# Second pass of layer one in pairs of blocks: 29 products on streamed weight sums in place of 2 × 15 on resident ones

## The chip, the cores and the metric

The kernel runs on one core of one Trainium2 chip. The core has five engines that run their own instruction streams: TensorE (PE in the profile, its weight loads PEld), VectorE (DVE), ScalarE (ACT), GpSimd (POOL) and SyncE (SP), which here issues the DMAs. Measured is the device time of one execution, in microseconds (us). The kernel before takes 2706.76 us, the median of three runs (2703.83, 2707.84, 2706.76).

## The reference

The input x has 128 batch entries of 64 tokens with 768 channels. It is normalised per token and cut at zero; two graph layers follow, and x is added at the end. All of it is fp32. One layer, with h the tokens and weights W_left, W_right, W_lin (768 × 768):

```python
m_left = h @ W_left.T;  m_right = h @ W_right.T          # per token
u_left = h @ m_left.T / sqrt(768); u_right = h @ m_right.T / sqrt(768)   # 64 x 64 per batch entry
u = u_left * adj_tri + u_left * diag_mask + u_right * adj_tri.T
e = exp(u) * adj;  attention = e / (sum(e, axis=2) + 1e-10)
h_lin = h @ W_lin.T + b_lin
ctx = attention @ h_lin
h = relu(layer_norm(ctx, ln_a, ln_b))       # (z - mean) / (std + 1e-3) * a + b
```

## The kernel before

The tokens are worked on in 16 blocks of 512 (8 batch entries), or 8 pairs of blocks. A block is held transposed, channels on partitions. The 768 channels are three thirds of 256, each of two halves of 128 partitions. Both dense multiplications are done by a scheme that trades products for sums: a block's 512 tokens are two groups of 256, the channels three thirds in and three out, and in place of all the small products the kernel multiplies sums of weight slices by sums of token groups. A product is one weight sum (256 × 256) times one token sum (256 tokens), which is several matmuls into a PSUM bank, and the bank is added to or subtracted from several outputs.

Each layer has two passes.

*Pass one* (`pass_one`, L436) makes `m_left` and `m_right`, the scores and the attention. It works in pairs of blocks: 29 products (`PRODUCTS`, L116) of each kind, left and right (`project`, L520; its matmuls are L535). The weight sums were made once (`W_OPS`, 23 sums beyond the nine raw slices) and stand in DRAM, from where SP streams them into a ring of eight tiles (`stream`, L198). Token sums (`X_OPS`, 30 per pair) are made by POOL (`token_op`, L277) four products ahead. VectorE and ScalarE read the banks (`read`, L295; the sums L222 and L223).

*Pass two* (`pass_two`, L847) makes `h_lin`, the context and the normalisation. It works in single blocks: 15 products each (`ORDER`, L97; `linear`, L1055, matmuls L1069), with weight sums of W_lin that stay in SBUF in the tile ROOM all through the pass (15 slots), and 11 token sums a block on POOL (`T_SUMS`, L92). The bias is copied into each block's first banks by ScalarE ahead of the products (`fresh`, L838). In layer one (l = 0 in the code) the context of blocks 0 to 12 is made by `context_block` (L881, 16 matmuls, L900, in one place, after the next block's product 12) and normalised by `finish_block` (L964); those of blocks 13 to 15, and all of layer two, are made in two halves in two places (`context`, L867, matmuls L877; `finish`, L1011). Since the mean is taken out of W_lin, b_lin and with it of ctx beforehand (`centre`, L201), the normalisation needs only the sum of squares (ScalarE), its root, and an inverse (VectorE). The rows z are stored to DRAM for the next pass.

*What sets the order.* The program is written out in the order of its loops, and each engine runs its instructions in that order. Work that is not TensorE's is put between products in two ways: `put` gives a function a slot (pass one has four slots per pair of left and right product, 116 for a pair of blocks; a block of pass two has 30), and `idle` is a queue from which `run` (L75) takes one function at each slot where the plan has none. A function of the queue may be `None`, for a pause. The last pair of pass one, U = 7 of 0 to 7, has the queue of `one_aside` (L1143): eight pauses, then nine loads of slices of W_lin by SP (`load_n`, L152 to L154, into ROOM), `centre` (nine reductions L216, means, nine subtractions L219, all on VectorE), and the 17 sums `W_SUMS` on POOL that turn nine slices into the 15 of `ORDER`. The last two softmax chains, of blocks 14 and 15, follow the end of the pair. Pass two of layer one has the queue of `two_aside` (L1151): the raw loads of W_left and W_right of layer two, their sums on POOL, and stores of them to DRAM (L196).

SP's queue holds in order: the streams of pass one, the loads of tokens (1.5 MB a block), attention (128 KB), stores of rows (192 KB each) and weight sums (256 KB each). A copy on ScalarE (L565) holds SP back in U = 7 until 795 us.

## Time and profile before

| what | value |
|---|---|
| median of the three runs | 2706.76 us |
| the profiled execution, device time | 2705.84 us |
| its span | 2704.1 us |
| its mean granted TensorE clock | 0.998 |
| pass one, layer one | 0 to 891.5 us, TensorE busy 879.38 |
| pass two, layer one | 891.5 to 1357.3 us, TensorE busy 464.69 of 465.80 |
| pass one, layer two | 1357.3 to 2222 us, TensorE busy 863.52 |
| pass two, layer two | 2222 to 2704.1 us, TensorE busy 470.10 |

In the lines of the profile each entry names the line of the code, the engine, the operation, and the tiles: `X<-room,ts` is a write to PSUM bank X from the weight tile room and a token sum. A duration in microseconds follows, or in groups the number of instructions (x...), the busy time and the mean duration in ns. The windows show, for a stretch, the busy time of each engine with its number of instructions, then the granted clock, the share of the DMA engines that was busy, and GB/s. The stages end at the first product of the next one.

### The profile page before, as it was taken

The page shows a single profiled execution, that of the slowest core. Times are in us where ns is not written, and L with a number is a line of the kernel's source. Part 1 is how long each engine was busy: PE and PEld are TensorE (multiplying, and loading weights), DVE is VectorE, ACT ScalarE, POOL GpSimd, SP SyncE. Part 2 cuts the span into 40 slices and gives each one's busy share as a digit, 9 for nine tenths or more (in the row PEclk, how much of TensorE's full clock was granted, in tenths as well). Part 3 has the DMA queues.
Part 4 walks back from the last instruction along what each step waited for, and adds up shares of the span by engine and source line. Part 5 has one row for each costly group of instructions (what it writes and reads, how often), then busy time and mean ns, then how long its engine had stood idle before and what let it go on. Part 6 is the DMA issues. An engine that isn't in the chain of part 4 may idle for free.

```text
span 2704.1 us, 47306 instructions
## 1 busy us (share of the span) xinstructions
PE 2677.7 (99%) x18514; PEld 2301.3 (85%) x18514; DVE 1499.1 (55%) x2456; ACT 832.4 (31%) x1617; POOL 1381.4 (51%) x1071
## 2 busy tenths in 40 slices
PE   9999999999999999999999999999999999999998
PEld 8788888888888888888788888888888888888886
DVE  7664755756647433334344545546446475666667
ACT  4032131221310254454631221221212304445443
POOL 6633244333336765566433325335244286887886
PEclk9999999999999999999999999999999999999999
DMA  8886956858765345558594956968759524655655
GB/s 272 268 309 212 289 197 208 279 202 265 244 207 181 102 143 184 166 167 255 184 284 174 317 187 212 286 191 279 229 193 301 211 79 135 182 160 159 186 154 148
DMA packets 310222, 567.81 MB, mean 210 GB/s; under 512 B 62832, under 2 KB 190064, under 8 KB 301808
## 3 DMA queue, kind: packets, MB, share of 16 engines
q1 hardware_dynamic: 309840, 564.39, 64.9%
q8 instruction: 148, 2.42, 0.4%
q14 instruction: 74, 0.61, 0.1%
q10 hardware_dynamic: 160, 0.39, 0.0%
HBM read 429.40 MB, written 135.27 MB: 209 GB/s over the span
## 4 chain that ended last, share of the span: by engine, by line
PE 96%; DVE 1%; SPq 0%; issue 0%; DMA 0%; ACT 0%; DVEq 0%; ACTq 0%
PE right L535 17%; PE X L1069 12%; PE X L535 11%; PE V L535 11%; PE Z L535 9%; PE Y L535 9%; PE V L1069 8%; PE Y L1069 6%; PE both L474 5%; PE Z L1069 4%; PE aux L877 2%; PE aux L900 1%; PE Y L900 0%; PE Z L474 0%; DVE wp L223 0%
## 5 line engine op out<-in xcount | busy, mean ns | idle before, releaser
L223 POOL TENSOR_TENSOR ts<-ht 128x512 f32<-128x512 f32 x352 | 481.6, 1374 | 172.6 <-PE X L1069 69.6
L223 POOL TENSOR_TENSOR ts<-ht,ts 128x512 f32<-128x512 f32 x192 | 252.9, 1324 | 345.7 <-PE V L535 202.1
L535 PE MATMUL right<-ts,wp 128*128 128x252 f32 (+1 forms) x1632 | 380.9, 376 | 0.6 <-DVE wp L223 0.6
L535 PEld LDWEIGHTS right<-ts,wp 128*128 128x128 f32 x1632 | 310.0, 190 | 39.5 <-DVE wp L223 1.0
L483 POOL TENSOR_TENSOR wm<-adj,tri 128x256 f32<-128x256 f32 x60 | 42.3, 728 | 490.7 <-DMA wp<-ws 274.5
L223 DVE TENSOR_TENSOR m<-m,X 128x512 f32<-128x512 f32 x160 | 105.5, 684 | 257.9 <-ACT m L305 180.2
L223 DVE TENSOR_TENSOR m<-m,right 128x504 f32<-128x504 f32 (+1 forms) x304 | 199.5, 674 | 87.8 <-PE right L535 74.1
L1069 PE MATMUL X<-room,ts 128*128 128x256 f32 x1024 | 244.0, 380 | 0.2
L535 PE MATMUL Z<-ts,wp 128*128 128x256 f32 x992 | 234.3, 379 | 0.0
L223 POOL TENSOR_TENSOR ts<-ht,ht 128x512 f32<-128x512 f32 x128 | 163.2, 1285 | 137.8 <-PE right L535 92.8
L1069 PEld LDWEIGHTS X<-room,ts 128*128 128x128 f32 x1024 | 191.7, 190 | 31.7 <-issue 1.8
L535 PEld LDWEIGHTS Z<-ts,wp 128*128 128x128 f32 x992 | 188.4, 190 | 24.9
L535 PE MATMUL X<-ts,wp 128*128 128x256 f32 x872 | 207.5, 381 | 1.9 <-DVE wp L223 1.9
L535 PE MATMUL V<-ts,wp 128*128 128x252 f32 (+1 forms) x864 | 201.6, 376 | 0.0
L305 ACT ACTIVATE m<-right 128x504 f32<-128x504 f32 (+1 forms) x64 | 36.2, 592 | 506.8 <-PE both L474 486.8
L535 PEld LDWEIGHTS X<-ts,wp 128*128 128x128 f32 x872 | 164.4, 190 | 25.5 <-POOL ts L223 2.3
L382 ACT ACTIVATE ht<-ht,b_col,a_col 128x512 f32<-128x512 f32 x192 | 141.3, 806 | 140.9 <-DMA ht<-h 140.9
L1069 PE MATMUL Y<-room,ts 128*128 128x256 f32 x768 | 182.5, 379 | 0.0
L535 PEld LDWEIGHTS V<-ts,wp 128*128 128x128 f32 x864 | 164.2, 190 | 20.4
L1069 PEld LDWEIGHTS Y<-room,ts 128*128 128x128 f32 x768 | 145.8, 190 | 20.4 <-issue 0.6
L223 DVE TENSOR_TENSOR hl<-hl,V 128x512 f32<-128x512 f32 (+1 forms) x136 | 89.2, 656 | 128.9 <-PE V L1069 118.7
L223 DVE TENSOR_TENSOR m<-m,Y 128x512 f32<-128x512 f32 x144 | 95.8, 684 | 116.0 <-PE Y L535 105.2
(225 smaller groups left out, 4866.3 us busy)
## 6 DMA issues: line engine op xcount, KB each, us to landing
wp<-ws SPq DMA_DIRECT2D x435, 512.0 KB, 6.3
ht<-h SPq DMA_DIRECT2D x62, 1536.0 KB, 8.3
h<-room SPq DMA_DIRECT2D x112, 384.0 KB, 7.1
z<-z SPq DMA_DIRECT2D x128, 192.0 KB, 3.1
ws<-wp SPq DMA_DIRECT2D x93, 256.0 KB, 4.2
xr<-in_x_dram SPq DMA_DIRECT2D x120, 192.0 KB, 3.6
out_dram<-xr SPq DMA_DIRECT2D x120, 192.0 KB, 2.6
room<-z SPq DMA_DIRECT2D x112, 192.0 KB, 5.1
```

The source lines that it names most:

```text
L223: (eng.tensor_add if sign == "+" else eng.tensor_sub)(o, a, b)
L305: nc.scalar.activation(to(o), p, AF.Copy, scale=1.0 if sign == "+" else -1.0)
L382: nc.scalar.activation(ht, ht, AF.Relu, bias=cols[1][:, c:c + 1], scale=cols[0][:, c:c + 1])
L474: nc.tensor.matmul(p[h * S + e:h * S + e + 32, q, e:e + 95], ht[:, c, b * S + e:b * S + e + 32], mb[:, e:e + 95], start=(c == 0), stop=(c ...
L483: nc.gpsimd.tensor_tensor(wm[:, :, k], adj[:, :, 1 - k], tri[:, k].unsqueeze(1).to_broadcast([P, Q, S]), op=ALU.mult)
L535: nc.tensor.matmul(p[:, g], wk[:, c, g * P:(g + 1) * P], tk[:, c, :].rearrange("p (b s) -> p b s", s=S)[:, :, :ns], start=(new and g == c ...
L877: nc.tensor.matmul(cx[k][i, m, :HH], at[j, q, :], hl[j, q, m * HH:(m + 1) * HH], start=True, stop=True)
L900: nc.tensor.matmul(parts[r, k][n][i], at[j, q, :], hl[j, q, cut], start=True, stop=True)
L1069: nc.tensor.matmul(p[:, n], b[t][:, c, r * P:(r + 1) * P], w[s][:, c, :], start=(i in FIRST and i not in PRELOAD and n == c == 0), stop=(c ...
```

## The change

In pass two of layer one, blocks 0 to 13 are worked on as seven pairs with 29 products each (`PAIRS`), the same scheme as in pass one but with its own order and signs; blocks 14 and 15 keep `linear` with the 15 old sums.

- *Weights.* The 29 weight sums are made in the last pair of pass one: `pair_weights` replaces `sums_n` in the queue. Its functions are, in order: nine stores of raw (centred) slices, 23 sums alternately on POOL and VectorE, each with a store to DRAM where `PAIRS` uses it (`WN`, 29 tiles of 256 KB), then the 17 old sums on POOL with a pause after each and stores of the 15 results (`WO`), then the first nine streams. The pauses ahead of the loads are ten rather than eight. With `both`, `run` takes from the queue at every slot of this pair, also where the plan has something; in the pairs it does so at every second product.
- *Streams.* ROOM becomes a ring of nine slots of 256 KB (`NR`); after product n SP issues the load for product n + 9. The last nine of these, and `first_weights` in the last pair, bring the old sums back for blocks 14 and 15.
- *Token sums.* 30 per pair on POOL (`PAIR_OPS`), eight products ahead, in place of 2 × 11.
- *First reads and bias.* VectorE does all reads of the pairs' banks; the first read of an output adds or subtracts the bias (`read_biased`), in place of ScalarE's copy ahead and its first reads.
- *Context.* `context_block` and `finish_block` are gone. Each pair makes the four halves of the two blocks before it after its products 0, 4, 9 and 14, with `context` and `finish`.
- *Places.* The loads of tokens, attention and rows, and the transposes for layer two, are put at other slots; `h_lin` has a third buffer in ROOM.

The diff, cut to its core:

```diff
-    def run(slot):
-        if slot in plan:
-            for f in plan.pop(slot):
-                f()
-        elif idle:
+    def run(slot, both=False):
+        given = plan.pop(slot, ())
+        for f in given:
+            f()
+        if idle and (both or not given):
             f = idle.popleft()
...
+    PAIR_OPS = ((2, 12, "-", 3, 11), (2, 13, "-", 12, 1), (4, 14, "-", 5, 4), (4, 15, "-", 1, 14),
...
+    PAIRS = ((9, 9, "X", True, "+1+5"), (11, 4, "Y", True, "-8"), (3, 13, "V", True, "-5"),
...
+    WN = {w: dram.tile([P, K2, D], F32, name=f"wn{w}") for w in sorted({p[0] for p in PAIRS})}
+    WO = [dram.tile([P, K2, D], F32, name=f"wo{s}") for s in range(len(ORDER))]
...
+    NR = 9
+
+    def stream_n(n):
+        nc.sync.dma_start(single(n % NR), WN[PAIRS[n % len(PAIRS)][0]])
+
+    def pair_weights(own):
...
+        def keep(w):
+            if w in WN:
+                nc.sync.dma_start(WN[w], where[w])
+
+        def sums(n, eng):
+            _, o, sign, a, b = W_OPS[n]
+            t = where[o] = spare.popleft()
+            if sign == "neg":
+                eng.tensor_scalar_mul(t, where[a], -1.0)
+            else:
+                added(eng, t, sign, where[a], where[b])
+            keep(o)
...
+        for w in range(9):
+            idle.append(lambda w=w: keep(w))
+        for n in range(len(W_OPS)):
+            idle.append(lambda n=n: sums(n, (nc.gpsimd, nc.vector)[n % 2]))
...
+        def old(n):
+            o, s, a, b = W_SUMS[n]
+            added(nc.gpsimd, single(o), s, single(a), single(b))
+            keep_old(n)
...
+        idle.append(lambda: keep_old(-1))
+        for n in range(len(W_SUMS)):
+            idle.extend([lambda n=n: old(n), None])
+        idle.append(None)
+        for n in range(NR):
+            idle.append(lambda n=n: stream_n(n))
...
-                            run(2 * n)
+                            run(2 * n, l == 0 and U == NU - 1)
...
+            def read_biased(p, to, sign, j):
+                b = rows["bias", l][:, (4, 2, 0)[j]].unsqueeze(1).to_broadcast([P, 2, D])
+                if j == 0:
+                    (nc.vector.tensor_add(to, p, b) if sign == "+" else nc.vector.tensor_sub(to, b, p))
...
+            def pair(s, ends):
+
+                late, seen, bank = [], set(), {}
...
+                for i, (w, t, at, new, what) in enumerate(PAIRS):
+                    if new:
+                        bank[at] = ps_st.tile([P, 2 * TH], F32, name=at)
+                    p = bank[at].rearrange("p (r d) -> p r d", r=2)
+                    x, wt = tokens(l, s, t, 2), single((s * len(PAIRS) + i) % NR)
+                    for r in range(2):
+                        for c in range(K2):
+                            nc.tensor.matmul(p[:, r], x[:, c, r * P:(r + 1) * P], wt[:, c, :],
+                                             start=(new and r == c == 0), stop=(c == K2 - 1), skip_group_check=True)
+                        if r == 0:
+                            run(2 * i, i % 2)
...
+                        if o in seen:
+                            added(nc.vector, to, sign, to, pp)
+                        else:
+                            read_biased(pp, to, sign, j)
...
+                    n = s * len(PAIRS) + i + NR
+                    if n < (NU - 1) * len(PAIRS):
+                        stream_n(n)
...
+            def first_weights():
+                t = sp.tile([P, H // 32, Q, 32], F32, name="xb", bufs=1).rearrange("p b q j -> p (b q j)")
+                W[l, "n"] = {}
+                for n in range(6):
...
+            def pairs():
+                for s in range(NU - 1):
+                    for n in range(2):
+                        put(4 + 10 * n, lambda n=n: load_h(2, l, 2 * s + 2 + n))
+                        put(40 + 3 * n, lambda n=n: load_at(2 * s + n))
+                    put_pair_ops(s, "after", PAIR_SLOTS)
...
+                    if s == NU - 2:
+                        put(30, first_weights)
+                    if s in aside:
+                        aside[s]()
+                    ends = {}
+                    if s:
+                        ends = {e: ((2 * s - 2 + n // 2, n % 2), (2 * e + 6, 2 * e + 7, 2 * e + 8))
+                                for n, e in enumerate((0, 4, 9, 14))}
+                    pair(s, ends)
...
-            idle.extend(none * 8)
+            idle.extend(none * (8 if l else 10))
             later(load_n(l), 0)
             centre(l)
-            later(sums_n(l), 0)
+            if l:
+                later(sums_n(l), 0)
+            else:
+                own = sp.tile([P, 2 * H], F32, name="own", bufs=1)
+                pair_weights([own[:, n * K2 * D:(n + 1) * K2 * D].rearrange("p (c d) -> p c d", c=K2) for n in range(3)])
```

## The prediction

> **What bounds the kernel now.** I read the page first, then the chain that ended last, then the stage in question by time windows.
>
> ```profile
> span 2704.1 us, 47306 instructions
> PE 2677.7 (99%) x18514; PEld 2301.3 (85%) x18514; DVE 1499.1 (55%) x2456; ACT 832.4 (31%) x1617; POOL 1381.4 (51%) x1071
> PE 96%; DVE 1%; SPq 0%; issue 0%; DMA 0%; ACT 0%; DVEq 0%; ACTq 0%
> ```
>
> TensorE works 99% of the span and carries 96% of the chain: a matmul saved is time saved, if everything that feeds it stays ahead. Second pass, layer one (L0 in the code), runs from 891.5 to 1357.3 us. Windows (columns: length, then PE, PEld, DVE, ACT, POOL busy, clock, DMA share, GB/s):
>
> ```profile
> 840.00:850.00 10.00, 10.00 (x48) 8.80 (x47) 10.00 (x14) 0.00 (x0) 8.24 (x7) 1.00 0.59 202
> 891.50:1357.30 465.80, 464.69 (x2435) 379.55 (x2432) 176.53 (x323) 220.74 (x543) 284.13 (x226) 1.00 0.56 177
> 1130.00:1140.00 10.00, 10.00 (x48) 8.74 (x47) 3.19 (x5) 1.69 (x3) 3.09 (x3) 1.00 0.97 316
> 1280.00:1290.00 10.00, 10.00 (x66) 7.18 (x65) 5.93 (x9) 3.01 (x5) 3.82 (x3) 1.00 0.99 341
> ```
>
> The stage has room on DVE, ACT and POOL on average, and 177 GB/s of DMA on average; but there are stretches of 10 us where the DMA engines are full, at 316 to 341 GB/s. The first line lies before the stage, at the end of pass one: VectorE is full there already. The timeline of TensorE gives the prices of a product and of a context:
>
> ```profile
> 1023.85 1.89 PE L1069 MATMUL Y<-room,ts 128*128 128x256 f32 x8
> 1025.58 1.89 PE L1069 MATMUL V<-room,ts 128*128 128x256 f32 x8
> 1027.40 0.65 PE L900 MATMUL Y<-hl,at 64*64 64x512 f32 x2
> 1028.31 1.90 PE L900 MATMUL aux<-hl,at 64*64 64x256 f32 x24
> 1030.14 1.99 PE L1069 MATMUL Z<-room,ts 128*128 128x256 f32 x8
> ...
> 2308.96 1.89 PE L1069 MATMUL X<-room,ts 128*128 128x256 f32 x8
> 2310.78 1.52 PE L877 MATMUL aux<-hl,at 64*64 64x384 f32 x16
> 2312.23 1.99 PE L1069 MATMUL Z<-room,ts 128*128 128x256 f32 x8
> ```
>
> A product (8 records of 4 fp32 matmuls) starts every 1025.58 − 1023.85 = 1.73 us. A whole-block context takes 1030.14 − 1025.58 = 4.56; with the product after it (1.83 to the next), less two products (3.45), it costs 2.94 per block. The two-place form, which layer two has at 2308.96: 3.27 + 1.83 − 3.45 = 1.65 a place, 3.30 per block.
>
> **The change part by part.**
>
> *Products.* Seven pairs take 29 products in place of 30: −7 × 1.73 = −12.1 us. All of it lies on the path.
>
> *Context.* Blocks 0 to 12 leave the block form for two places: 13 × (3.30 − 2.94) = +4.7. Blocks 13 to 15 had two places already.
>
> *End of pass one, the part that decides.* In the last pair's run (U=7, starting about 784; a step, one kind of one product, is 1.73 us, 58 steps) the old kernel loads nine slices of W_lin, centres them and makes 17 sums on POOL. The new one makes 23 further weight sums, alternately on POOL and VectorE, each stored by SP, then the 17 old ones, each of the 15 survivors stored, then nine streams. It takes work from the idle queue at every slot, so the centring is pulled forward: to steps 12 to 21 from 823–862 us. The relevant rows:
>
> ```profile
> L154 SPq DMA_DIRECT2D room<-in_w_lin_dram x9: 367/384/537, 775.6 to 818.4; - x9
> DMA to landing us min/median/max: 2.7/8.3/10.7
> L219 DVE TENSOR_TENSOR room<-room,wmm x9: 679/850/1780, 838.7 to 861.2; 128x512 f32<-128x512 f32 x9
> PE Z L1069 <- DVE wp L490: 1.1, 2, 0.6
> ```
>
> VectorE between steps 12 and 38 (26 × 1.73 = 45 us): reads of PSUM 26 × 0.62 (the spacing of its reads) = 16; two blocks' softmax pieces 6.5; centring nine reduces at 0.68, nine subtractions (9.4 together in this trace, 0.68 to 1.78 each), three means, 18 with their gaps; 11 weight sums at 1.05 (the nine subtractions' mean, as they too run beside POOL) 11.5. Sum 52. Waits in order: the first reduces stand at step 12, about 804, while SP, held by a copy until 795, issues its slices at about 1 us each until 803.5, and they land 8.3 later: about 4 lost. The alternating sums make DVE wait for POOL and back: some 3. So 58 against 45, 13 behind. Reads of PSUM queue behind this on VectorE, and TensorE waits for the banks that they free: the banks let it run 2 or 3 steps (3 to 5 us) ahead, so it is about 9 late. Lower bound 0 (subtractions at 0.68, slices landing in 2.7: demand 45); upper 13.
>
> That lateness moves POOL too. From the end of the VectorE jam (about 862) POOL still owes the 17 old sums, the last 8 or so token sums of U=7, seven of the first pair and two blocks' masks: 33 × 1.23 (spacing of its sums in the row of 17) = 40 less what overlaps: the last old sum ends about 898. In the kernel before it ended at 893.8 and TensorE began pass two at 891.5, waiting only 0.6 for Z. Now the first streamed weight stands on SP behind the store of that last sum, and lands 4 later (a 256 KB store's 4.2, below): product 0 at about 902 against 891.5 = +10.5, less the small gap at 894 that goes (Z at 894.09, 1.73 after X would be 893.27: 0.8, of which 0.7 is taken): +9.8. The lateness in pass one is within this, not beside it. Ends: −0.7 (POOL and SP done by 888), +20 (VectorE's whole 13 reaches product 0, and 7 more of POOL's and SP's queues).
>
> *Weights from DRAM.* A product now needs a stream of 256 KB.
>
> ```profile
> wp<-ws SPq DMA_DIRECT2D x435, 512.0 KB, 6.3
> ht<-h SPq DMA_DIRECT2D x62, 1536.0 KB, 8.3
> ws<-wp SPq DMA_DIRECT2D x93, 256.0 KB, 4.2
> z<-z SPq DMA_DIRECT2D x128, 192.0 KB, 3.1
> ```
>
> One pair lasts 29 × 1.73 + 4 × 1.65 = 56.7 us and moves 29 × 256 KB of streams, two loads of 1.5 MB, 16 stores of 192 KB, attention, plus what the weight work of layer two does at that time: by my count of the issues 17.7 MB in pair 1, 20.5 in pair 2, 18.4 in pair 3, 14.6 in 4 and 5. At 315 GB/s, the full windows' rate (316, and up to 341), they take 57.4, 66.6 and 59.9: 0.7 + 9.9 + 3.2 = 13.8 behind at the end of pair 3. A stream is issued after product n for n + 9, 8 products and a context ahead (15.5), less 4 for landing: 11 of slack. So +3 to +3.5 of waits in pair 3; I take +3.5. Ends: 0 (341 GB/s: 53.0 + 61.5 + 55.4, some 5 behind), 15 (290, the worst rate of the windows with stores of 192 KB: 62.4 + 72.4 + 65.0 is 25 to 30 behind).
>
> The Trainium skill, page "DMA: Bandwidth & Descriptors", section "Bandwidth", asks to batch transfers to 1 MiB or more for three quarters of the peak; streams of 256 KB go against it. In this trace a 1.5 MB load lands in 8.3 us, 190 KB per us, and a 256 KB one in 4.2, 62 KB per us, so rows and page agree in direction; but several are in flight at a time, and the windows of mixed sizes still reach 316 to 341 GB/s. By the page alone the sum would have a stall near the upper end, 15 in place of 3.5.
>
> *Covered, at nothing.* POOL: 30 token sums × 1.28 = 38 per 56.7 us in place of 2 × 11 × 1.28, with about 12 weight sums 54: just enough, a lag of 10 is caught by its 8 products ahead (14); without cover each missed sum is 1.28. VectorE reads 41 × 0.69 = 28 of 56.7 per pair; the first reads leave ScalarE, which loses the bias preloads too. The normalisation behind a context has a chain of squares, root and inverse; the two places' slots leave it 5.2 us, the root took 2.5. SP: 77 issues × 0.6 = 46 of 56.7 us, so a late store can push streams; that is in the range. Block 14's first weights (6 into a free tile at slot 30, 9 into the ring) are loaded a product's worth at a time in the last pair (20 MB, 8 us behind at 315, under the slack of 11).
>
> *Sum.* −12.1 + 4.7 + 9.8 + 3.5 = +5.9. The profiled execution took 2705.84 with a span of 2704.1, 0.9 under the median of 2706.76; on the median, +5.9 gives 2712.7, taken as 2713. About 0.2% (5.4 us) is what a measurement of this kernel can tell from no change.
>
> **The rivals.**
>
> 1. *The tail of pass one is free, and the streams too (not slower).* If VectorE keeps up, subtractions at 0.68 as the fastest in the row and slices landed by 806, then its demand is 45 in 45 and product 0 starts where it did. For it: DVE is at 55% over the span, and POOL has idle time in 845–855 (5.61 busy of 10). Against it: 840–850 is full on VectorE already, without the added sums. Price: −12.1 + 4.7 − 0.7 = −8.1, so 2699. It decides if VectorE's lag stays under the 3 to 5 us of the banks.
> 2. *Tail free, streams cost 3.5 to 5.* The DMA engines do fall behind in pairs 2 and 3, though pass one did not: −8.1 + 3.5 to 5, 2702 to 2704; say 2703, no change that can be measured.
> 3. *Streams starved.* The engines give 290 GB/s with many small packets and SP's stores lie between: 25 behind less 11 is 14 of stall, in place of 3.5: 5.9 + 10.5, about 2723; twice that if pairs 4 and 5 do not catch up, 2740. For it: windows at 0.97 to 1.00 share before the streams exist. Against: 290 is the worst I found in windows of 5 to 10 us, not a mean over a pair.
>
> That the change doesn't do what it says is excluded: it has 28 matmuls less on TensorE.
>
> **How the numbers follow.** Forecast (tail +9.8, streams about 3.5) 0.38; rival 3, 0.12; rival 2, 0.18; rival 1, 0.32. Slower: 0.38 + 0.12 = 0.50; same 0.18; faster 0.32 (rival 1 is 8 below, just beyond 0.2%). The range: from 2699, the middle of rival 1, which leaves about 0.13 below, to 2728, which leaves the worse half of rival 3 above. The forecast's own range is 2706 to 2722.
>
> **What would show it.** In the changed profile: TensorE's first product of pass two near 902 (rival 1 and 2: 891); VectorE full from about 805 to 862 and TensorE waiting on its reads there; the product's pace still 1.73 and 29 per pair, contexts at 1.65 a place; waits of TensorE for the ring's loads in pairs 2 and 3, 3 to 4 us together (rival 3: 14 or more), none in pairs 4 and 5; POOL's token sums never what TensorE waits for in pairs. I am wrong if TensorE waits for POOL in the pairs, or if the store or load of a context's rows on SP holds a stream back for longer than 11 us.

## The result, and the profile after

The changed kernel takes 2730.17 us (median of five runs, 2728.26 to 2732.16) against 2706.76: a ratio of 1.009, 95% interval 1.0075 to 1.0104. It is 23 us slower; 2713 was forecast, with 2728 as the upper end of the range.

The page of the kernel after: span, engines, chain.

```profile
span 2726.1 us, 47585 instructions
PE 2682.3 (98%) x18458; PEld 2293.3 (84%) x18458; DVE 1575.3 (58%) x2575; ACT 746.2 (27%) x1334; POOL 1465.9 (54%) x1139
PE 90%; DVE 2%; POOL 2%; DMA 2%; issue 1%; ACT 1%; SPq 0%; DVEq 0%; POOLq 0%; ACTq 0%
```

TensorE's share of the chain fell from 96 to 90%; DMA, POOL and VectorE now have 2% each. The span is 22.0 us longer although 28 matmuls are gone. TensorE's waits before the first product of pass two, and then behind it (what it waited for; total, times, longest in us):

```profile
PE Y L628 <- DVE m L247: 2.5, 1, 2.5
PE X L1114 <- DMA room<-wn: 2.4, 1, 2.4
PE right L628 <- DVE m L247: 1.8, 2, 0.9
PE Y L628 <- POOL wm L576: 1.7, 1, 1.7
PE Z L628 <- POOL room L247: 1.0, 1, 1.0
...
PE Y L1114 <- DMA room<-wn: 3.6, 2, 1.8
PE aux L974 <- ACT z L1072: 3.5, 6, 0.9
PE Z L1114 <- DMA room<-wn: 3.0, 2, 2.7
```

The timeline of TensorE at the start of pass two, in pair 0, in pair 6 and in block 15:

```profile
903.94 2.40 PE L1114 MATMUL X<-room,ht 128*128 128x256 f32 x8 [2.42 <-DMA room<-wn]
906.13 3.19 PE L1114 MATMUL Y<-room,ht 128*128 128x256 f32 x8
909.15 1.89 PE L1114 MATMUL V<-room,ts 128*128 128x256 f32 x8
...
936.11 1.99 PE L1114 MATMUL Y<-room,ht 128*128 128x256 f32 x8 [1.73 <-DMA room<-wn]
...
1286.20 2.37 PE L1114 MATMUL Z<-room,ht 128*128 128x256 f32 x8 [2.69 <-DMA room<-wn]
1288.36 3.21 PE L1114 MATMUL V<-room,ts 128*128 128x256 f32 x8
1291.41 1.89 PE L1114 MATMUL X<-room,ht 128*128 128x256 f32 x8
...
1344.84 2.30 PE L974 MATMUL aux<-room,at 64*64 64x384 f32 x16 [0.90 <-ACT z L1072]
```

A product takes 1.73 from start to start, but the two behind the wait of 2.42 take 2.19 and 3.02, and the two behind the wait of 2.69 take 2.16 and 3.05. The windows say why (length, then busy time and instructions of PE, PEld, DVE, ACT, POOL, then the granted clock, DMA share, GB/s): the clock drops to 0.56 some 2 us after each of these two waits, for about 3 us.

```profile
906.00:909.15 3.15, 3.15 (x9) 2.48 (x9) 3.05 (x5) 0.00 (x0) 3.15 (x3) 0.56 0.94 340
1288.40:1291.40 3.00, 3.00 (x9) 2.43 (x8) 1.28 (x2) 0.00 (x0) 0.00 (x0) 0.56 0.82 267
```

**Where the 22 us are.** The last long group of scores in the last pair of pass one begins at 788.80 before and 788.04 after, ahead of all that the change touches; times are counted from it, since executions differ by up to 4 us in what comes earlier. The lines of this group and of the last long group, before and then after:

```profile
788.80 4.13 PE L474 MATMUL both<-m,ht 128*32 128x95 f32 x192
882.84 4.13 PE L474 MATMUL both<-m,ht 128*32 128x95 f32 x192
```

```profile
788.04 4.13 PE L567 MATMUL both<-m,ht 128*32 128x95 f32 x192
892.47 4.13 PE L567 MATMUL both<-m,ht 128*32 128x95 f32 x192
```

To the last group: 94.0 before, 104.4 after, +10.4. To the first product of pass two: 102.7 before, 115.9 after, +13.2. Pass two: 465.8 before (891.54 to 1357.34), 474.75 after (903.94 to 1378.69), +8.95. All that follows: +0.6; the earlier part −0.8. The forecast's own terms for pass two without its stall give −12.1 + 4.7 and the first gap of 0.5: −7.9. Against that stand the slow products at the start (0.46 + 1.29 over the pace, 1.75), pair 0's waits with what is slow behind them (0.51 + 0.29 + 1.89 = 2.7), pair 6's (2.85 + 0.43 + 1.32 + 1.99 = 6.6), and the contexts in the last two blocks (by the starts of TensorE's groups they take 7.0 over the pace, waits of 3.5 and slower matmuls behind them; the kernel before has 1.3 of that too: 5.7): 16.75 in all, which leaves 0.1 without a name.

### The profile page after: what moved, and what is told of

It is laid out like the page before. It is cut to its first block, busy times and chain, and to the rows that moved or that the text cites. A ratio compares the mean times of both kernels' runs of the same rounds, so it can differ in the third digit from the quotient of the medians.

```text
span 2726.1 us, 47585 instructions
## 1 busy us (share of the span) xinstructions
PE 2682.3 (98%) x18458; PEld 2293.3 (84%) x18458; DVE 1575.3 (58%) x2575; ACT 746.2 (27%) x1334; POOL 1465.9 (54%) x1139
## 3 DMA queue, kind: packets, MB, share of 16 engines
q8 instruction: 148, 2.42, 0.4%
## 4 chain that ended last, share of the span: by engine, by line
PE 90%; DVE 2%; POOL 2%; DMA 2%; issue 1%; ACT 1%; SPq 0%; DVEq 0%; POOLq 0%; ACTq 0%
PE right L628 16%; PE X L628 10%; PE V L628 10%; PE Z L628 8%; PE Y L628 8%; PE X L1200 7%; PE both L567 4%; PE V L1200 4%; PE Y L1114 3%; PE aux L974 3%; PE X L1114 3%; PE Y L1200 3%; PE Z L1114 3%; PE V L1114 3%; PE Z L1200 2%; POOL room L247 1%
## 5 line engine op out<-in xcount | busy, mean ns | idle before, releaser
L247 POOL TENSOR_TENSOR ts<-ht 128x512 f32<-128x512 f32 x303 | 418.1, 1385 | 103.1 <-PE right L628 48.5
L247 POOL TENSOR_TENSOR ts<-ht,ht 128x512 f32<-128x512 f32 x191 | 243.8, 1284 | 170.9 <-PE right L628 92.7
L475 ACT ACTIVATE ht<-ht,b_col,a_col 128x512 f32<-128x512 f32 x192 | 140.7, 803 | 138.6 <-DMA ht<-h 138.6
L1054 ACT ACTIVATE z<-aux 128x768 f32<-128x768 f32 x126 | 101.0, 807 | 230.8 <-PE aux L974 214.5
L1067 POOL TENSOR_TENSOR z<-z,b 128x768 f32<-128x768 f32 x62 | 112.7, 1830 | 89.8 <-DVE z L1064 89.8
L247 POOL TENSOR_TENSOR ts<-ts,ht 128x512 f32<-128x512 f32 x110 | 141.5, 1287 | 13.8 <-PE V L628 8.3
L628 PE MATMUL right<-ht,wp 128*128 128x252 f32 (+1 forms) x624 | 146.2, 378 | 0.0
L247 DVE TENSOR_TENSOR m<-m,V 128x504 f32<-128x504 f32 (+1 forms) x160 | 104.4, 677 | 71.9 <-PE V L628 60.8
```

Of the source, the lines that this page charges most:

```text
L247: (eng.tensor_add if sign == "+" else eng.tensor_sub)(o, a, b)
L475: nc.scalar.activation(ht, ht, AF.Relu, bias=cols[1][:, c:c + 1], scale=cols[0][:, c:c + 1])
L628: nc.tensor.matmul(p[:, g], wk[:, c, g * P:(g + 1) * P], tk[:, c, :].rearrange("p (b s) -> p b s", s=S)[:, :, :ns], start=(new and g == c ...
L1054: nc.scalar.activation(zs[k].rearrange(two, n=2), cx[k], AF.Square, accum_out=ss[:, k:k + 1])
L1067: nc.gpsimd.tensor_add(zs[k], zs[k], rows["b"])
```

## The experiments

All edits are to the changed kernel. "First product" is counted from those scores. Device times are of one execution, but for the runs with a ratio, the kernel before and the changed kernel (medians).

| run | first product | pass two | device |
|---|---|---|---|
| before | 102.7 | 465.8 | 2706.8 |
| changed | 115.9 | 474.8 | 2730.2 |
| new sums left out | 107.1 | 476.8 | 2723.3 |
| old sums left out | 113.1 | 478.4 | 2733.5 |
| layer two's weights from pair 1 | 115.4 | 472.7 | 2725.8 |
| affine operations apart | 115.8 | 473.5 | 2728.1 |
| rows, both in pair 4 | 115.4 | 478.0 | 2732.9 |
| centring in the order 1, 0, 2 | 110.3 | 476.8 | 2723.9 |
| own chains for POOL and VectorE | 116.3 | 478.9 | 2733.6 |
| five changes together | 109.5 | 489.0 | 2735.1, ratio 1.0107 (1.009 to 1.0124) |
| the same, root's addition on ScalarE | 112.2 | 479.9 | 2729.7 |
| rows apart, pairs 4 and 5 | 115.6 | 468.4 | 2723.4 |
| eight changes, with own chains | 111.5 | 469.8 | 2721.0, ratio 1.0055 (1.0038 to 1.0071) |
| six changes, alternating sums | 109.2 | 467.2 | 2718.0, ratio 1.004 (1.0026 to 1.0054) |
| the six, old sums left out | 109.2 | 469.1 | 2718.6 |
| the six, new sums left out | 104.1 | 470.9 | 2715.5 |

In five executions whose code up to the first product is the changed kernel's, the first product stands at 115.4 to 115.9. The two with five changes, alike up to there, differ by 2.8. So differences of under 3 us between the times of single runs are not leaned on below; what is smaller is read from waits at their place in the trace.

### New sums left out

```diff
-            idle.append(lambda n=n: sums(n, (nc.gpsimd, nc.vector)[n % 2]))
+            idle.append(None)
```

with the streams reading the seven raw slices that are stored.

> Left out of the changed kernel: the 23 new weight sums in the last pair of pass one and the stores of their results; the streams of the pairs read the raw slices that were stored (numbers wrong, sizes and count of the transfers the same). In the changed kernel the first product of pass two starts at 903.94 us against 891.54, TensorE having waited 7.7 us in U = 7 and run slowly for 2 to 3 more. Theory A (VectorE and POOL, which wait for each other over the alternating sums, hold TensorE's banks): waits of TensorE in U = 7 fall to at most 3 us (the raw slices' late landing stays), no wait for the first stream, first product at 893 to 897, device time 2718 to 2722. Rival B (the centring pulled forward does it, the sums fit in): first product still at 900 or later, device time within 3 us of 2730.

Theory A holds for the start: 107.1, 8.8 earlier, and the waits of TensorE behind VectorE and POOL between 846 and 856 are gone; two of 0.9 and 1.0 near 830 stay. The device time, 2723.3, missed the range of 2718 to 2722: it gained only 7, as pair 0 now waits 3.30 and 0.60 for streams, in place of 0.35 and 1.73.

### Old sums left out

```diff
             o, s, a, b = W_SUMS[n]
-            added(nc.gpsimd, single(o), s, single(a), single(b))
             keep_old(n)
```

> Left out of the changed kernel: the additions of the 17 old sums (their stores stay, so blocks 14 and 15 get wrong weights). Theory A: POOL is relieved of 17 x 1.23 = 21 us after 866 us, but TensorE's lateness was made before that, so only the 2.4 us wait for the first stream and the slow products behind it (1.8) go: first product at 900 to 902, device time 2725 to 2727. Rival C (POOL's backlog sets the start, as the prediction's step had it: last old sum, store, stream): first product at 893 to 896, device time near 2719.

The start gains 2.8, the wait for the first stream: A, and not what the prediction had as the step that decides. Up to the last scores this run and the changed kernel agree (104.7 and 104.4), though POOL is done sooner: SP issues the first streams 93.7 us after the scores in place of 111.6. The device time missed, at 2733.5: waits for streams grew to 3.1 in pair 0 and 6.3 in pair 6, and this execution was 2.9 late before the scores.

### Layer two's weights from pair 1 on

```diff
-    pass_two(0, {0: two_aside()})
+    pass_two(0, {1: two_aside()})
```

> The loads and sums for layer two's weights begin one pair later (pair 1 in place of pair 0). Theory D (pair 0's two waits for streams come from the nine raw loads that SP issues between streams in its first 30 us, DMA at 345 to 406 GB/s there): no wait of TensorE between 905 and 960, 2.7 us less with the slow product; but pair 1 now has raw loads on top of the streams, and may wait there up to 3 us if DMA is what matters; device time 2727 to 2728 if it does not. Rival E (the streams are late because the first nine started late and SP is behind the attention's stores): the waits in pair 0 stay, device time 2730.

Theory D: no wait in pair 0 behind the first stream's, 2.1 less in pass two. Pair 6 keeps waits of 5.1 in three places. The raw loads between the streams are what starved pair 0.

### Affine operations apart

```diff
-                        put_all(14, affine(1, 1, 0) + affine(1, 1, 1))
+                        put_all(14, affine(1, 1, 0) + affine(1, 1, 1), 3)
```

> The 12 affine operations on ScalarE for layer two's first pair (0.72 us each) stand at every third slot of blocks 14 and 15 in place of every slot from 14 on. TensorE waits 3.5 us in six places there for ScalarE's scaling of the context before, with the matmuls behind it slower. Theory F (the affine operations stand ahead of the scaling in ScalarE's queue): these waits fall to under 1.5 us, the stage is 2 to 4 us shorter, device time 2726 to 2728. Rival G (the four places are simply too near to each other, 4 products, for squares, root, inverse and scaling): the waits stay, device time 2730.

Between the two: the waits in six places, 3.5, became 1.8 in three, 1.2 less in pass two. The timeline of ScalarE in the changed kernel shows both parts, the affine operations (L475) ahead of and between the scalings (L1072):

```profile
1329.38 4.32 ACT L475 ACTIVATE ht<-ht,b_col,a_col 128x512 f32<-128x512 f32 x6
1333.61 0.36 ACT L940 COPY X<-bias 128x256 f32<-128x256 f32 x1
1333.92 0.81 ACT L475 ACTIVATE ht<-ht,b_col,a_col 128x512 f32<-128x512 f32 x1
1334.63 0.88 ACT L1072 ACTIVATE z<-aux,rs 128x768 f32<-128x768 f32 x1
```

The waits that stay are in block 15, which is made in two halves: its products take 0.86 us, so the contexts stand closer in time. The kernel before has one such wait there too, of 0.45. That the places are too close (G) for what stays was not tested by itself.

### Rows of layer two's first blocks, both in pair 4

```diff
-                    for u, slot in ((NB - 5, 29), (NB - 4, 0)):
-                        if u // 2 == s:
+                    for u, at, slot in ((0, 4, 0), (1, 4, 29)):
+                        if at == s:
```

> The row loads, transposes and stores of layer two's first two blocks (they come from blocks 0 and 1, long done) move from pairs 5 and 6 to pair 4, where the DMA engines have room (249 GB/s). Theory H (pair 6 has too many bytes: streams, tokens, rows, transposed stores and the six loads of old sums; DMA share 0.97, and 1.0 with 400 GB/s before the wait): the two waits of TensorE for streams in pair 6 (2.7 and 1.8 us, 6.6 with the slow products behind them) go, stage end 5 to 7 us earlier, device time 2723 to 2725; pair 4 shows no new wait. Rival J (it is SP, held by the stores of rows that wait for ScalarE): the first wait stays at 2 us or more, device time 2728 or more.

Neither. Pair 6 had no wait, but pair 4 got one of 4.62, at 1185.84. The windows of this run ahead of it:

```profile
1175.00:1180.00 5.00, 5.00 (x25) 4.39 (x24) 2.61 (x5) 0.00 (x0) 4.09 (x4) 1.00 1.02 215
1180.00:1185.00 5.00, 1.22 (x6) 0.74 (x4) 3.01 (x4) 0.00 (x0) 1.26 (x1) 0.86 1.04 235
```

The DMA engines are full at 215 to 235 GB/s, behind eight row loads of 192 KB and the stores of z. So it is not the pair's bytes (H) that count; the rows fill the engines with few bytes. Each row load goes to 32 of the 128 partitions of its tile (L463); whether that is the reason was not tested. SP, too, issued no stream while the row loads went out (1172.4 to 1178.9). Whether the full engines or SP's order made the stream late, this run does not separate.

### Rows apart, one block in each of pairs 4 and 5

```diff
-                    for u, slot in ((NB - 5, 29), (NB - 4, 0)):
-                        if u // 2 == s:
+                    for u, at in ((NB - 5, 4), (NB - 4, 5)):
+                        slot = 29
+                        if at == s:
```

> The changed kernel with the rows of layer two's first two blocks half a pair or a pair earlier, one block in each of pairs 4 and 5 (slot 29 in both; the changed kernel has them at slot 29 of pair 5 and slot 0 of pair 6; both in pair 4 moved the wait there, 4.6 us at a DMA share of 1.0 with only 215 to 235 GB/s). Theory H2 (what fills the DMA engines are the row loads and the stores beside them, which move few bytes for the time that they take; two blocks' worth one after the other starve the streams, one block's worth does not): no wait of TensorE for a stream over 1 us in pairs 4, 5 and 6, device time 2723 to 2726. Rival O (any block's rows starve the streams by 2 us or more): waits of 2 us or more behind each, device time 2728 or more.

H2: no wait for a stream in pairs 1 to 6, pass two 6.4 us shorter, 2723.4. The six loads of old sums still stand together at slot 30 of pair 6, and are harmless there.

### Centring in the order of the loads

```diff
-        for j in range(3):
+        for j in (1, 0, 2):
...
-            idle.extend(none * (4 if j == 0 else 0))
+            idle.extend(none * (4 if j == 1 else 0))
```

> The thirds of W_lin are centred in the order 1, 0, 2 in place of 0, 1, 2: the first three slices that SP loads are those of third 1, while those of third 0 are loads 4, 7 and 8. In the changed kernel VectorE waits for them 4.2 and 1.9 us from 804 on. Theory K (the prediction's term, some 4 us lost to late slices): these waits fall under 1.5 us, TensorE's waits near 830 and 834 (2.6) go, the first product comes 2 to 3 us earlier against the scores at 788, device time 2726 to 2728. Rival L (the time is lost later anyway, in the alternating sums and POOL's queue): first product within 1 us of where it was.

K, and more: 5.6 us. VectorE's waits in the changed kernel between 800 and 900, and below them the first line of those with the order changed:

```profile
DVE wm L240 <- DMA room<-in_w_lin_dram: 6.0, 2, 4.2
DVE room L247 <- POOL room L247: 5.5, 2, 3.7
```

```profile
DVE room L247 <- POOL room L247: 5.5, 2, 3.7
```

The wait for the slices is all but gone (0.6 in one place), the wait for POOL is the same. Of the 5.6, TensorE's waits are 3.0: the 2.6 near 830 and 834 go, and behind the alternating sums 4.0 stay of 4.4. The other 2.6 are products that ran below the pace in the changed kernel. There the clock stood at 0.55 from 847 to 849.75, behind a wait of 2.46; here it stayed at 1.00 behind a wait of 2.73. Why it did is not known, so the order of the loads is worth the 3.0 of waits, and what it does to the clock may be chance.

### Own chains for POOL and VectorE

```diff
+        by_vector = (12, 15, 16, 23, 26, 27, 18, 29, 30, 31, 28)
+        first = [op for op in W_OPS if op[1] not in by_vector]
+        second = [next(op for op in W_OPS if op[1] == o) for o in by_vector]
+        ops = [x for n in range(12) for x in (first[n:n + 1] + second[n:n + 1])]
```

and `ops` in place of `W_OPS`.

> The same 23 new sums, 12 on POOL and 11 on VectorE, but shared out so that each engine's sums read only raw slices and its own results; the two lists alternate in the queue. Theory M (VectorE stands 3.7 and 1.8 us waiting for POOL's sums between 839 and 850, and TensorE 4.4 behind it plus 2 to 3 at the lower clock): these waits go, the first product comes 4 to 7 us earlier against the scores at 788, device time 2722 to 2726. Rival N (POOL's amount of work sets the start): TensorE is earlier in U = 7 but waits longer for the first stream, the first product moves by less than 2 us.

N by the number (116.3 after 115.9), but not by its reason: TensorE does not wait for the first stream. It no longer waits in 846, but 3.95 for a token sum of POOL at 872.72. In the changed kernel POOL waits 4.6 for VectorE's sums in this stretch; here it waits 6.8 in three places for the store of a weight sum whose tile it is to write again:

```profile
POOL room L247 <- DMA wn<-room: 3.9, 2, 2.6
POOL own L247 <- DMA wn<-own: 2.9, 1, 2.9
```

The last of these, 2.63, stands one sum ahead of the token sum. So the edit took one wait away and made another, as the new order of the sums uses the tiles again sooner. What the dependence between the engines costs by itself, this run does not show.

### Five changes together

The order of the centring, own chains, layer two's weights from pair 1, rows in pair 4, the six loads and the affine operations apart: six edits, which the recorded texts call the five changes. Beside the edits above:

```diff
-                    nc.sync.dma_start(to, WO[ORDER[n][0]])
+                    put(32 + 4 * n, lambda n=n, to=to: nc.sync.dma_start(to, WO[ORDER[n][0]]))
```

> Together: centring in the order 1, 0, 2; own chains for POOL and VectorE; layer two's weights from pair 1 on; rows of blocks 0 and 1 in pair 4; the six loads of old sums one at a time (slots 32 to 52); the affine operations at every third slot. If the causes named for the 22 us (13.2 up to the first product, 9 behind it) are right and independent, some 3 to 5 us remain at the start and 2 in the last blocks against the -7.9 that the fewer products less the contexts and the first gap give: 2704 to 2709 us, no change against before that can be measured. Rival: the causes take each other's place (a wait removed moves to the next), and it stays at 2715 or more.

The rival. At the start the changes help (109.5); in pass two new waits appear, 4.9 and 4.7 behind the rows as above, and one of 6.7 for a context. VectorE before that one:

```profile
1020.36 0.69 DVE L1101 TENSOR_TENSOR room<-Z,bias 128x512 f32<-128x512 f32 x1 [1.04 <-PE Z L1118]
1020.97 10.04 DVE L1063 TENSOR_SCALAR rs<-sd 128x2 f32<-128x2 f32 x1
1031.05 0.17 DVE L1064 RECIPROCAL rs<-rs 128x2 f32<-128x2 f32 x1
```

An addition to 256 numbers took 10.04 us. In that time POOL made eight sums with no gap, and it was done when POOL paused, at 1030.99. All other TENSOR_SCALARs of this line, in all traces, take 0.13 to 1.27.

### The same, with the root's addition on ScalarE

```diff
                 nc.scalar.activation(sd, ss, AF.Sqrt, bias=floor, scale=1.0 / (H - 1.0))
+                nc.scalar.activation(sd, sd, AF.Identity, bias=eps_ln)
...
-                    nc.vector.tensor_scalar_add(rs, sd, EPS_LN)
-                    nc.vector.reciprocal(rs, rs)
+                    nc.vector.reciprocal(rs, sd)
```

> The run with five changes together, with one more: the addition of 1e-3 to the root, a TENSOR_SCALAR of 128x2 on VectorE, is made by ScalarE. In that run one such instruction took 10.04 us while POOL made eight sums without a gap, and TensorE waited 6.7 us for the context behind it. Theory P (this form of VectorE instruction can't start while POOL's sums follow each other without a gap): the 10 us and the wait of 6.7 go, the reciprocal in its place takes 0.17, device time 2735 less 7 to 9, 2726 to 2728. Rival Q (VectorE stands there for something else, a semaphore or code): another instruction at that place takes as long, device time 2733 or more.

P for the wait: it is gone, the reciprocal takes 0.15 although POOL again makes its sums without a gap there, and pass two is 9.1 shorter. The device time stands at 2729.7 as the first product came 2.8 later than in the run without this edit.

### Eight changes, with own chains

The order, own chains, these six old sums on VectorE, 16 pauses ahead of the raw loads in pair 0, rows apart, six loads apart, affine apart, and a context of block 15 later:

```diff
         def begin():
+            idle.extend(none * 16)
             for kind in "lr":
...
-            added(nc.gpsimd, single(o), s, single(a), single(b))
+            added(nc.vector if n in (4, 5, 6, 7, 15, 16) else nc.gpsimd, single(o), s, single(a), single(b))
...
-                        ends = ({1: ((u - 1, 0), (13, 14, 16))
+                        ends = ({4: ((u - 1, 0), (13, 14, 16))
```

> Together: centring in the order 1, 0, 2; own chains of new sums for POOL and VectorE, and six of the 17 old sums (again a chain that reads only raw slices and its own results) on VectorE; 16 pauses ahead of layer two's raw loads in pair 0; rows apart as in the run with that name; the six loads of old sums one at a time (slots 32 to 52); the affine operations at every third slot; the first context of block 15's first half after product 4 in place of 1. If the start is bound by POOL's amount of work (its last sum, store, first stream), taking 7 us from POOL brings the first product to 104 to 107 us after the scores at 788 (102.7 before, 115.9 changed, 109.4 in the run with five changes); with 1 to 3 us of waits left behind it the device time is 2699 to 2707. Rival: VectorE's queue is late now, with TensorE behind it in U = 7: 110 or more, device time 2710 or more.

The rival's numbers for the start, 111.5, but not its place: TensorE waited 3.79 for POOL's token sum at 869.54, 0.9 for VectorE, and 2.27 ahead of the last scores, for which the profile names no releaser. The end of POOL's work did come sooner: SP issued the first streams 98.7 us after the scores, against 106.5 in the run with five changes, and TensorE did not wait for them. So POOL's last sum was not what set the start here. The token sum in the middle was late, as POOL had stood 1.90 for a store of a weight sum and its sums beside VectorE's take longer. POOL's sums in this run, while VectorE makes sums in SBUF and later, while it makes none:

```profile
848.11 1.72 POOL L247 TENSOR_TENSOR room<-room 128x512 f32<-128x512 f32 x1
849.91 1.73 POOL L247 TENSOR_TENSOR own<-room 128x512 f32<-128x512 f32 x1
...
890.48 1.28 POOL L247 TENSOR_TENSOR ts<-ht,ts 128x512 f32<-128x512 f32 x1
891.72 1.28 POOL L247 TENSOR_TENSOR ts<-ht 128x512 f32<-128x512 f32 x1
```

### Six changes, alternating sums

The last list without the own chains and without old sums on VectorE.

> The changes that helped one by one, without the own chains: centring in the order 1, 0, 2; 16 pauses ahead of layer two's raw loads; rows apart in pairs 4 and 5; old sums loaded one at a time; affine operations at every third slot; block 15's first context after product 4. Against the scores at 788 the first product came at 110.3 with the order alone, pass two took 468.4 with the rows apart alone. If the causes add up: first product at 109 to 111, pass two 461 to 465 (no wait in pair 0, 4, 5 or 6 above 1 us, 1 to 2 us in the last blocks), device time 2711 to 2715: better than the changed kernel by 15 to 19, still slower than before by 5 to 8, which is the start. Rival: the waits move as in the run with five changes, 2721 or more.

The start came as expected, 109.2; pass two, 467.2, stays 2 above the range, with waits of 0.7 in pair 0, 1.1 for a token sum, 0.9 and 1.2 in pair 3, 1.5 and 0.5 in the last blocks. It is the best of the versions that leave nothing out, 12 us faster than the changed kernel and still 0.4% slower than before. No version beat the kernel before.

### The six, old sums left out; the six, new sums left out

> The same with the 17 old sums left out (their stores stay; blocks 14 and 15 get wrong weights): 21 us less for POOL in U = 7. Left out of the changed kernel alone they brought 2.8 us at the start, because VectorE's lateness lay before them. Theory R (with the centring in order what is left of the start is POOL's amount of work, new sums, old sums and token sums): first product at 103 to 106, device time 2706 to 2710. Rival S (it is the alternating new sums alone): first product at 108 or later, device time 2711 or more.

> The run with the six changes of order and place, with the 23 new sums and the stores of their results left out (streams read the raw slices that were stored; numbers wrong, transfers of the pairs the same). With them the first product comes 109.2 us after the scores at 788, without the old sums too. Theory T (the new sums, 12 on POOL and 11 on VectorE, beside the reads are all that is left of the late start): 102.5 to 104.5, device time 2706 to 2710. Rival U (the centring between steps 12 and 21, which the kernel before has later, keeps a part): 106 or more.

S and T for the start: without the 17 old sums nothing moves (109.2), without the 23 new ones it is 104.1. The new sums cost 5.1 of the 6.4 that the start is late, the rest is within the spread of single runs. Both device times missed, at 2718.6 and 2715.5: TensorE came earlier and waited for streams in pair 0 (2.6 and 2.4, the second with slow products behind) and in pair 3 (3.0 and 3.1).

## Why the prediction was wrong

The forecast's sum was −12.1 + 4.7 + 9.8 + 3.5; the span says +22.0 in place of +5.9. The first two terms hold. The steps that failed are these: the streams, put at 3.5 in pair 3, cost 9.3 in pairs 0 and 6; the contexts of blocks 14 and 15, covered by the list at nothing, cost 5.7; the start, put at 9.8 (10.5 less a gap of 0.7), cost 13.2; and the slow products behind the first wait, 1.75, had no term. With the start taken against the 10.5, these four are 16.0 of the 16.1 that are missing.

- *Products and context: right.* A pair without waits takes 56.66 (from the context at 960.48 to the one at 1017.14), 56.7 by the prediction, against 57.68 for two blocks before. Seven times the difference is 7.1, near the forecast's 7.4.
- *End of pass one: right in kind, its parts not.* Forecast was a first product at 902, +9.8; it came at 903.9. POOL's end came as forecast, its last old sum at 899.2 (898 by the prediction) and the first stream 4.7 later. The step that failed is that this backlog sets the start and that TensorE's lateness lies within it: leaving the old sums out brings 2.8, since TensorE alone was 10.4 late. That 10.4 stands so near the forecast's 9 is partly luck. It is 7.0 of waits and 3.4 of products below the pace, which the sum did not have. VectorE's parts missed both ways: it waited 6.0 for the slices (about 4 by the prediction) and 5.5 for POOL (3), its 11 weight sums took 15.2 (11.5), the nine subtractions 6.6 (9.4). The prediction had named the loads but not that third 0's slices are loads 4, 7 and 8.
- *Weights from DRAM: mis-sized and misplaced.* Forecast: 3.5 in pair 3, because the engines give 315 GB/s (the 13.8 less 11 of the working are 2.8, not 3 to 3.5, and the 4.2 us of a 256 KB transfer are those of a store; a streamed sum lands in 4.8). In pair 2 they gave 364 and pairs 1 to 5 had no wait. Pairs 2, 3, 5 and 6:

```profile
1017.20:1073.80 56.60, 56.60 (x297) 45.75 (x296) 29.19 (x49) 14.84 (x28) 54.43 (x45) 1.00 1.01 364
1073.80:1130.70 56.90, 56.90 (x297) 45.66 (x296) 28.80 (x49) 14.84 (x28) 51.98 (x42) 1.00 0.93 324
1187.40:1244.00 56.60, 56.60 (x297) 45.78 (x296) 32.89 (x53) 14.73 (x28) 37.70 (x31) 1.00 0.90 284
1244.00:1307.40 63.40, 58.88 (x300) 46.84 (x299) 32.51 (x53) 15.47 (x29) 37.94 (x32) 0.97 0.97 318
```

  The waits came to 9.3 with the slow products, in pair 0, where streams and raw loads share SP and the engines, and in pair 6. The sum over a pair of bytes by one rate was the wrong view: it is a stretch of 10 to 15 us ahead of a product that matters, and row traffic fills it at 215 to 235 GB/s. The kernel before shows this rate already. Its eight row loads keep SP for 11.46 us, and with them under way the engines are full at 219 GB/s; the prediction's "290 is the worst I found" had overlooked it:

```profile
1192.54 11.46 SPq L370 DMA_DIRECT2D x<-z  x8
1200.00:1205.00 5.00, 5.00 (x44) 2.85 (x43) 1.98 (x3) 2.69 (x10) 4.54 (x5) 1.00 0.98 219
```

- *Covered, at nothing: one entry was not covered.* "The two places' slots leave it 5.2 us" holds in the pairs. In blocks 14 and 15, ScalarE has 12 affine operations and its first reads in the same queue, and the change puts four contexts at every fourth product there: 5.7 us. Spreading the affine operations took 1.2 of it away. The prediction looked at the pairs alone.
- *POOL's token sums: right.* TensorE does not wait for them in the pairs, although POOL is busy 52 to 56 of 56.7 us in pairs 1 to 3.
- *The clock was not in the sum.* Behind the waits of 2.42 and 2.69 two products cost 1.75 together; that is 3.5 in pass two. Behind 1.73 and 1.83 there is no such loss. In other runs some waits of 2.4 to 2.8 have it and some do not (last section).

The rivals: none was this. Rival 3 had the sign and a near time (2723), by starved streams in the pairs in general. What happened is a late start, as in the forecast but later, plus starved streams in two places, plus contexts in the last blocks.

## What to carry to other kernels

A stage at 99% of TensorE has little to win by fewer products (7 us of 2707) and pays for each thing that its new inputs disturb: go through the first and last part of the changed stage by themselves, since the middle was as computed. Look at the order in which loads land against the order in which they are used, and at each prefetch against the worst 10 us ahead of it, by the share of the DMA engines and not by bytes. Removing one wait often brought the next: causes worth 1 to 6 us alone gave 12 together in one combination and lost 5 in another.

## What was not expected of the hardware

- *VectorE and POOL hold each other up on sums in SBUF.* A VectorE sum of 128x512 tiles in SBUF takes 0.65 to 0.69 while POOL is idle and up to 1.79 beside POOL; POOL's take 1.27 alone and 1.7 beside VectorE. Two of VectorE's in the changed kernel, the first in a stretch in which POOL does nothing (815 to 825), the second while it makes sums:

```profile
819.79 0.69 DVE L243 TENSOR_TENSOR room<-room,wmm 128x512 f32<-128x512 f32 x1
842.92 1.74 DVE L247 TENSOR_TENSOR room<-room 128x512 f32<-128x512 f32 x1 [3.74 <-POOL room L247]
```

  It is also what spread the subtractions' times in the kernel before (0.68 to 1.78), which the prediction took as the price wherever they stand; those of 0.68 and 0.69 stand where POOL makes no sum. Pulled forward they took 0.68 to 0.69, but for one of 1.32 beside POOL.
  VectorE's reads of PSUM (0.68) are not touched. So the sums put on VectorE to relieve POOL take POOL's time too: one part of why the runs with own chains gained little, beside POOL's waits for stores. The Trainium skill, page "SBUF — State Buffer", section "SBUF: two separate sides", says that VectorE and GpSimd share a port pair under an exclusive lock, held for a whole instruction, for VectorE instructions with two SBUF inputs or in a two-port mode. The durations agree with it: 1.74 is the 0.65 of a sum alone and most of one POOL sum of 1.27.
- *The waiting engine can starve.* By that page the one that starts first gets the pair for the whole instruction. The TENSOR_SCALAR of 10.04 us let eight POOL sums pass. That it is this lock, and that this instruction is one of those that the page names, was argued from the times; shown is that with another instruction in its place the 10 us go.
- *The clock can fall after a short wait.* 2.42 us without matmuls were enough for a granted clock of 0.56 over 3 us, soon after. The length alone does not decide: behind waits of 2.61 (the six, old sums left out) and 2.81 (old sums left out) it stayed at 1.00. Between 780 and 1400 us of all runs, by the pace of the products that follow, no wait of up to 2.40 that stood alone brought it down, of those from 2.42 to 2.81 some did, and every one from 2.84 on did. The window behind the 2.61:

```profile
921.00:924.46 3.46, 3.46 (x17) 3.05 (x17) 0.69 (x1) 0.00 (x0) 1.27 (x1) 1.00 1.02 429
```

  The Trainium skill, page "TensorE: Matmul & The Clock Gate", section "What's actually happening", gives an idle window of about 3.4 us for it; here it sometimes took less.
